# An AdaLN layer with spectral attention and routed experts on one core: sequences' constants from diagonal products, and row statistics and an epsilon moved to the activation engine

## The chip, the core and the metric

The kernel runs on one core of a Trainium2 chip. The engines are TensorE (PE: matrix products; PEld is its weight load), VectorE (DVE), ScalarE (ACT), GpSimd (POOL) and SyncE (SP, whose queue issues transfers). The metric is the time of one launch in microseconds on the device; the profile is of one execution of its own.

## The reference

The inputs are x of 4 sequences x 1024 tokens x 256 features, all float32. In short:

```python
mod = (silu(c) @ wmod).reshape(4, 6, 1, 256)          # sa, ca, ga, sb, cb, gb per sequence
ga, gb = (sign(g) * maximum(abs(g), 0.25) for g in (ga, gb))
h = layernorm(x) * (1 + ca) + sa
q, k, v = (unit(h @ W.T + b) for W, b in (...))       # unit(y): ifft(f / (|f| + 1e-8)), f = fft(y)
s = cumsum(ifft(fft(k) * fft(v)).real, axis=1)        # over the tokens of a sequence
x = x + ga * ifft(fft(s) * conj(fft(q))).real
h = layernorm(x) * (1 + cb) + sb
gate = h @ gate_w                                     # 8 experts, the best 2, softmax of their values
x = x + gb * sum(weight_e * expert_e(h))              # expert: clipped swiglu of 256 -> 2 x 512 -> 256
```

## The kernel before, in words

Transforms are products with a real 256 x 256 matrix (`fwd`: cosines, sines, the two real bins). They are folded into the weights: `gmat` is a weight times `fwd`, and what depends on a sequence (modulation, gates) is folded into a wide tile of constants for each of the four sequences, `batch` (2856 columns on 128 partitions). It has the projections of keys, values and queries with gate columns (`KV`, `Q`), the inverse transform with the gate `ga` in its columns (`INV`), and rows that are the same on all partitions: gate additions (`LOG`), `sb`, `1 + cb`, and `gb` times the experts' second bias (`SB`, `CB`, `GB2`). The first two sequences' tiles are filled in place. For the last two a tile `of` is filled, written to DRAM (`kept`, 1428 KB) and loaded later into one of the two `batch` buffers. `project_of` fills the projections, `gates_of` the rest; a row of `gb` also goes to `kept_gb`, from which expert blocks gather.

Tokens are worked through in 8 groups of 4 x 128 (`GT`), two groups a sequence, each group as two pairs of 2 x 128 (`PT`). `begin_group` takes the mean and variance of each row (`moments`: bn_stats and bn_aggr on DVE, then a square root on ACT and a reciprocal). `pair` is a generator of eight steps: normalise (`xn`) and transpose; project (L528) and square; magnitudes (`mag`: sum of two squares, square root, plus epsilon) and the product of keys and values; the queries' magnitudes; the running sum by products with a triangular matrix (L569 to L579); the product with the queries and a transpose (L594); the inverse transform (L604), the addition to x (L612), the second row statistics; and normalised rows into `row`. Two pairs are in work at a time. `route(g)` ranks the gates, finds each row's two slots (`slot_i`), and scatters rows into expert order in DRAM with eight indirect transfers on POOL's queue (L715); then it writes the group's first sums to the output (L737 to L746). `row` has two buffers, the x tiles three. `plan` makes blocks of 256 rows of one expert out of the slots that are full; `Block` loads rows and first weights, turns the rows (L881), and runs the expert (L918 to L962). The first block is started after group 2 is planned; blocks are then mixed with the remaining groups at a set rate.

The constants of sequence 0 stand before the first group. Those of the others are emitted by `prepare_later`, one step at every second step of the main loop from step 8 on (`LATER`), so between the pairs of groups 1 and on. PSUM has eight banks: three of tag `gv` (expert blocks), one `y`, and in `ps_m` two `in`, one `mid` and one `late`, which the constants share with the pairs.

The program text is not the order of an engine's queue: the tile framework's scheduler orders each engine's instructions when the program is built, by its own estimates and the data's order. Each engine then works through its queue strictly in that order, and waits there for what an instruction needs.

Of the kernel before, what the change touches and what calls it, by code (L numbers as in the profile page):

```python
# [7 lines left out]
FP = mybir.dt.float32  # L8
I32 = mybir.dt.int32
AF = mybir.ActivationFunctionType  # L10
ALU = mybir.AluOpType
AX = mybir.AxisListType

P = 128
# [5 lines left out]
GN = GT * P  # L20
RESERVE = 4
RARE = 2
LATER = 8
# [14 lines left out]
def adaln_layer_kernel(  # L38
# [56 lines left out]
    def late():  # L95
        return bank("late")

    x_tiles = {}

# [13 lines left out]
    eps_ln = const.tile([P, 1], FP, name="eps_ln")  # L113
    nc.gpsimd.memset(eps_ln, LN_EPS)
    tiny = const.tile([P, 1], FP, name="tiny")
    nc.gpsimd.memset(tiny, 1e-30)
# [77 lines left out]
    fwd = sp.tile([P, 2, D], FP, name="fwd")  # L194
    bwd = sp.tile([P, 2, D], FP, name="bwd")
    bq = sp.tile([P, 3, 2], FP, name="bq")
# [68 lines left out]
    )  # L265
    silb = sp.tile([P, 2, BATCH, P], FP, name="silb")

# [3 lines left out]
    gate_inv = sp.tile([P, 2, BATCH, NE], FP, name="gate_inv")  # L271
    gate_add = sp.tile([P, BATCH, NE], FP, name="gate_add")

    def gate_constants():
        pm = late()
        pmv = pm[:, : 6 * BATCH].rearrange("p (w h b) -> p w h b", w=3, h=2)
        for w in range(3):
            for h in range(2):
                for k in range(2):
# [6 lines left out]
                    )  # L286
        col = sp.tile([P, 3, 2, BATCH], FP, name="col")
        nc.vector.tensor_copy(col, pmv)
        size = sp.tile([P, 2, BATCH], FP, name="col_size")
        raw = col[:, 0]  # L290
# [42 lines left out]

    def project_of(b, t):


        rows_of = sp.tile([P, 2, P], FP, tag="rows_of", name="rows_of", bufs=2)
        nc.vector.tensor_copy(rows_of, lift[:, :, b : b + 1].to_broadcast([P, 2, P]))
        pu = bank("mid").rearrange("p (t n) -> p t n", n=D), bank("late")
        for n in range(3):  # L340
            u = pu[0][:, n - 1, :] if n else pu[1][:, :D]
            for h in range(2):
                nc.tensor.matmul(
                    u, lhsT=rows_of[:, h, :], rhs=gmat[:, h, n, :], start=(h == 0), stop=False
                )
            for k in range(2):
                nc.tensor.matmul(u, lhsT=bb[:, n, k], rhs=fwd[:, k, :], start=False, stop=(k == 1))
        for h in range(2):
            nc.vector.scalar_tensor_tensor(
                t[:, h * HC + KV : h * HC + Q].rearrange("p (t n) -> p t n", n=D),  # L350
                gmat[:, h, 1:3, :], mod[:, 1, h, b : b + 1], pu[0],
                ALU.mult, ALU.add,
            )
        for h in range(2):
            nc.vector.scalar_tensor_tensor(
                t[:, h * HC + Q : h * HC + Q + D], gmat[:, h, 0, :], mod[:, 1, h, b : b + 1],
                pu[1][:, :D],
                ALU.mult, ALU.add,
            )

    def gates_of(b, t):

        pg = late().rearrange("p (n d) -> p n d", n=2)
        for n, at in enumerate((2, 5)):
            for k in range(2):
                nc.tensor.matmul(
                    pg[:, n, :],
                    lhsT=silb[:, k, b, :],
                    rhs=wm[:, k, at * D : (at + 1) * D],
                    start=(k == 0),  # L370
                    stop=(k == 1),
                )
        raw = sp.tile([P, 2, D], FP, tag="raw", name="raw", bufs=1)
        nc.scalar.copy(raw, pg)
        size = sp.tile([P, 2, D], FP, tag="size", name="size", bufs=2)
        nc.vector.scalar_tensor_tensor(size, raw, -1.0, raw, ALU.mult, ALU.max)
        nc.vector.tensor_scalar(raw, raw, 0.0, 2.0, ALU.is_ge, ALU.mult)
        nc.vector.tensor_scalar(raw, raw, -1.0, None, ALU.add)
        nc.vector.scalar_tensor_tensor(size, size, 0.25, raw, ALU.max, ALU.mult)
        inv = t[:, INV:LOG].rearrange("p (c n) -> p c n", n=IC)  # L380
        nc.vector.tensor_mul(
            inv[:, :, :D], bwd, size[:, 0, :].unsqueeze(1).to_broadcast([P, 2, D])
        )
        nc.vector.tensor_copy(inv[:, :, D:], gate_inv[:, :, b, :])
        nc.vector.tensor_copy(
            t[:, : 2 * HC].rearrange("p (h n) -> p h n", n=HC)[:, :, 3 * D :], gate_in[:, :, b, :]
        )
        nc.vector.tensor_copy(t[:, LOG : LOG + NE], gate_add[:, b, :])
        pg = late()
        for k in range(2):  # L390
            nc.tensor.matmul(
                pg,
                lhsT=silb[:, k, b, :],
                rhs=wm[:, k, 3 * D : 5 * D],
                start=(k == 0),
                stop=(k == 1),
            )
        nc.scalar.copy(t[:, SB : SB + D], pg[:, :D])
        nc.vector.tensor_scalar(t[:, CB : CB + D], pg[:, D:], 1.0, None, ALU.add)
        nc.vector.tensor_mul(t[:, GB2 : GB2 + D], b2_sb, size[:, 1, :])  # L400
        nc.sync.dma_start(out=kept_gb[b : b + 1, :], in_=size[0:1, 1, :])

    t0 = batch_tile(0)
    project_of(0, t0)


    share = sp.tile([P, 2], FP, name="share")
    nc.vector.tensor_scalar(share, ident[:, 0 : P : P - 1], -1.0 / D, 2.0 / D, ALU.mult, ALU.add)
    pt = bank("in", 2).rearrange("p (c n) -> p c n", c=2)
    for c in range(2):  # L410
        for k in range(2):
            nc.tensor.transpose(
                pt[:, c, k * P : (k + 1) * P], fwd[:, k, c * P : (c + 1) * P], ident
            )
    for c in range(2):
        nc.scalar.activation(bwd[:, c, :], pt[:, c, :], AF.Copy, scale=share[:, c : c + 1])
    nc.vector.tensor_copy(silb, sil.unsqueeze(3).to_broadcast([P, 2, BATCH, P]))
    gate_constants()
    gates_of(0, t0)
    nc.vector.tensor_sub(strict, triu, ident)  # L420
# [8 lines left out]
    def prepare(b):  # L429

        t = sp.tile([P, COLS], FP, tag="of", name="of")
        project_of(b, t)
        gates_of(b, t)
        nc.sync.dma_start(out=kept[:, b], in_=t)

    def deviations(mv, tag):

        n = mv.shape[1]
        root = two.tile([P, n], FP, tag=tag + "root", name="root")
        r = two.tile([P, n], FP, tag=tag + "r", name="rstd")  # L440
        nc.scalar.activation(root, mv[:, :, 1], AF.Sqrt, bias=eps_ln)
        nc.vector.reciprocal(r, root)
        return root, r

    def moments(src, tag):
# [6 lines left out]
        for i in range(n):  # L452
            nc.vector.bn_aggr(mv[:, i, :], st[:, i, :])
        return mv

# [24 lines left out]
    def begin_group(g):  # L480

        x4 = x_tiles[g]
        mv = moments(x4, "a")
        root, r = deviations(mv, "a")
        nmr = two.tile([P, GT], FP, tag="nmr", name="nmr")
        nc.vector.tensor_mul(nmr, mv[:, :, 0], r)
        nc.vector.tensor_scalar(nmr, nmr, -1.0, 1.0, ALU.mult, ALU.add)
        gate = two.tile([P, GT, NE], FP, tag="gate", name="gate")
        row = rows.tile([P, GT, ROW], FP, tag="row", name="row")
        nc.gpsimd.tensor_copy(  # L490
            row[:, :, D + NE :].bitcast(I32),
            numbers[:, g * GT : (g + 1) * GT, :],
        )
        of_group[g] = root, r, nmr, gate, row

    def pair(g, j):
# [48 lines left out]
        def magnitudes(lo, hi, eng):  # L545
# [6 lines left out]
            nc.scalar.activation(mag[:, :, lo:hi, :], mag[:, :, lo:hi, :], AF.Sqrt, bias=tiny)  # L552
            nc.vector.tensor_scalar(mag[:, :, lo:hi, :], mag[:, :, lo:hi, :], EPS, None, ALU.add)

        magnitudes(1, 3, nc.vector)
        nc.vector.tensor_mul(mag[:, :, 1, :], mag[:, :, 1, :], mag[:, :, 2, :])
        nc.vector.reciprocal(mag[:, :, 1, :], mag[:, :, 1, :])
# [42 lines left out]

        po = bank("mid"), late()
        for k in range(PT):
            for h in range(2):
# [7 lines left out]
        for k in range(PT):  # L611
            nc.vector.tensor_add(xp[:, k, :], po[k][:, :D], xp[:, k, :])  # L612

# [3 lines left out]
            )  # L617
        mv2 = moments(xp, "b")
        _, r2 = deviations(mv2, "b")
        yield  # L620

# [5 lines left out]
        nmr2 = two.tile([P, PT], FP, tag="nmr2", name="nmr2")  # L627
        nc.vector.scalar_tensor_tensor(nmr2, mv2[:, :, 0], -1.0, r2, ALU.mult, ALU.mult)
        h_row = row[:, j : j + PT, :D]
        for k in range(PT):  # L630
# [386 lines left out]
    def prepare_later():  # L1017

        nonlocal mone, mtwo, tiny_ones, loads, slot_rows
        t1 = batch_tile(1)  # L1020
        project_of(1, t1)
        yield
        gates_of(1, t1)
# [20 lines left out]
    for t in range(NG * PER + STEPS - HALFWAY + 3):  # L1044
# [42 lines left out]
        if done_now is not None:  # L1087
            routes.append([done_now, 0, route(done_now)])
        if t >= LATER and t % 2 == 0:
            next(later, None)  # L1090
# [90 lines left out]
```

## Time and profile before

| | us |
|---|---|
| median of 3 runs | 809.25 (808.28 to 811.38) |
| the profiled execution | 811.83 |
| its span | 809.9 |
| PE busy | 694.5 (86%) |
| DVE busy | 554.7 (68%) |
| ACT busy | 326.8 (40%) |
| POOL busy | 390.7 (48%) |
| group 0, 1, 2: slots known | 100.7, 146.35, 194.97 |
| first expert block turned | 210.7 |

Busy times are shares of the whole span, and the kernel has two parts with different limits: until about 211 us it makes constants and works on four groups of tokens, after that it works on experts and the other four groups. So a share is to be read by stretch. In rows of groups of instructions, "x8 | 14.1, 1757 | 0.0" means eight instructions, 14.1 us in all, 1757 ns each, and the idle time of the engine before them, with what ended it. An arrow `<-` in such a row stands between what is written and what is read. In rows by time the first two numbers are start and length in us.

### The profile page before, as it was taken

How to read it: one execution, taken by the hardware profiler on the slowest of the kernel's cores; microseconds unless marked ns; L12 is line 12 of the kernel's file. 1: busy time of each engine (PE TensorE's matmuls, PEld its weight loads, DVE VectorE, ACT ScalarE, POOL GpSimd, SP SyncE). 2: the span in 40 equal slices, each digit the busy share in tenths (PEclk: the TensorE clock that was granted, in tenths of full speed). 3: DMA queues.
4: the chain of work that ended last, by engine and by line, in shares of the span. 5: the costliest groups of instructions: out<-in, count | busy, mean ns of one | idle time of the engine just before them, and what ended most of it. 6: DMA issues, size and time to landing. Idle time of an engine off the chain costs nothing. (4 is left out here: it accounts for less than half of the span.)

```text
span 809.9 us, 10038 instructions
## 1 busy us (share of the span) xinstructions
PE 694.5 (86%) x2876; PEld 533.6 (66%) x2876; DVE 554.7 (68%) x1570; ACT 326.8 (40%) x606; POOL 390.7 (48%) x391
## 2 busy tenths in 40 slices
PE   6989796596697879799899897979968999999991
PEld 5655553353475657677587675758756888888881
DVE  3678979869366767878697867766925656655650
ACT  4435336153364626464566363534211332232230
POOL 1023143414354664666567656646755545555432
PEclk9989999585599879999899898989978999999996
DMA  9300041310762248327532752275876655755422
GB/s 312 131 0 1 18 174 60 122 57 32 237 179 53 47 124 284 79 54 219 130 84 61 228 133 31 69 207 140 168 217 175 143 144 165 181 166 168 91 40 26
DMA packets 55553, 100.16 MB, mean 124 GB/s; under 512 B 7165, under 2 KB 40586, under 8 KB 54986
## 3 DMA queue, kind: packets, MB, share of 16 engines
q1 hardware_dynamic: 38218, 72.68, 26.4%
q0 software_dynamic: 17280, 26.83, 18.9%
q8 instruction: 25, 0.41, 0.2%
q14 instruction: 30, 0.25, 0.1%
HBM read 72.80 MB, written 27.99 MB: 124 GB/s over the span
## 5 line engine op out<-in xcount | busy, mean ns | idle before, releaser
L918 PE MATMUL gv<-xt,w 128*128 128x256 f32 x1184 | 281.9, 392 | 11.8 <-DVE gt L930 7.8
L918 PEld LDWEIGHTS gv<-xt,w 128*128 128x128 f32 x1184 | 228.9, 197 | 48.3 <-DVE gt L930 9.6
L962 POOL DMA_INDIRECT out_dram<-gb,token x74 | 120.1, 1624 | 61.9 <-DVE gb L958 45.2
L948 PE MATMUL py<-w_sb,h 128*128 x592 | 137.2, 385 | 1.0 <-DVE gb L958 1.0
L901 POOL DMA_INDIRECT gb<-kept_gb,token x74 | 81.0, 1094 | 105.7 <-DVE gt L930 28.2
L934 ACT ACTIVATE sg<-gt 128x512 f32<-128x512 f32 x74 | 46.6, 630 | 206.2 <-DVE gt L930 169.2
L948 PEld LDWEIGHTS py<-w_sb,h 128*128 128x128 f32 x592 | 112.9, 192 | 18.0 <-DVE gb L958 1.4
L528 PE MATMUL in<-batch,ht 128*128 128x512 f32 (+1 forms) x256 | 99.1, 534 | 5.8 <-ACT ht L516 5.8
L715 POOL DMA_INDIRECT slots<-row,slot_i x64 | 67.3, 1052 | 51.5 <-DVE slot_i L710 24.3
L930 DVE TENSOR_SCALAR gt<-gv,bias 128x256 f32<-128x256 f32 x148 | 65.0, 474 | 24.0 <-PE gv L918 18.1
L528 PEld LDWEIGHTS in<-batch,ht 128*128 128x128 f32 x256 | 50.0, 205 | 44.0 <-issue 30.9
L942 POOL TENSOR_TENSOR h<-vt,sg 128x512 f32<-128x512 f32 x42 | 55.1, 1316 | 49.4 <-DVE vt L941 40.6
L937 ACT ACTIVATE vt<-gv,bias 128x256 f32<-128x256 f32 x148 | 61.5, 463 | 16.9 <-PE gv L918 15.6
L940 DVE TENSOR_SCALAR vt<-vt 128x512 f32<-128x512 f32 x74 | 34.2, 462 | 45.9 <-ACT vt L937 42.3
L547 POOL COPY mag<-sq 128x4 f32<-128x4 f32 (+1 forms) x64 | 21.3, 390 | 79.6 <-ACT sq L537 69.1
L941 DVE TENSOR_TENSOR vt<-vt,gt 128x512 f32<-128x512 f32 x74 | 51.9, 701 | 1.6
L958 DVE SCALAR_TENSOR_TENSOR gb<-py,weight,gb 128x256 f32<-128x256 f32 x74 | 32.7, 476 | 25.0 <-PE py L948 16.5
L535 ACT COPY z<-in 128x512 f32<-128x512 f32 (+1 forms) x64 | 29.5, 479 | 49.6 <-PE in L528 46.6
L563 POOL TENSOR_TENSOR z<-z,mag 128x512 f32<-128x512 f32 x16 | 20.6, 1284 | 47.2 <-DVE mag L562 36.0
L594 PE MATMUL mid<-msk,u 128*128 128x128 f32 x64 | 14.1, 328 | 31.9 <-DVE u L472 23.8
L737 PE MATMUL late<-batch,w_t 8*128 8x256 f32 x64 | 23.8, 502 | 15.1 <-ACT w_t L733 8.9
L451 DVE BATCH_NORM_STATS2 st<-x 128x6 f32<-128x256 f32 x64 | 24.3, 412 | 17.2 <-DMA x<-in_x_dram 17.2
(213 smaller groups left out, 1006.6 us busy)
## 6 DMA issues: line engine op xcount, KB each, us to landing
w<-in_w1t_dram SPq DMA_DIRECT2D x37, 1024.0 KB
x_in<-slots SPq DMA_DIRECT2D x37, 266.0 KB
x<-in_x_dram SPq DMA_DIRECT2D x8, 512.0 KB
w_sb<-in_w2t_dram SPq DMA_DIRECT2D x1, 4096.0 KB
out_dram<-x SPq DMA_DIRECT2D x8, 512.0 KB
kept<-of SPq DMA_DIRECT2D x2, 1428.0 KB
batch<-kept SPq DMA_DIRECT2D x2, 1428.0 KB
slots<-fill SPq DMA_DIRECT2D x9, 266.0 KB
```

Source lines behind the costliest of these rows:

```text
L528: nc.tensor.matmul(pz, lhsT=ht[:, h, k * P : (k + 1) * P], rhs=pb[:, h * HC + lo : h * HC + hi], start=(h == 0), stop=(h == 1),)
L715: s = nc.gpsimd.indirect_dma_start(out=slots, out_offset=bass.IndirectOffsetOnAxis(ap=slot_i[:, n, i : i + 1], axis=0), in_=row[:, i, :], ...
L901: nc.gpsimd.indirect_dma_start(out=self.gb[:, i, :], out_offset=None, in_=kept_gb, in_offset=bass.IndirectOffsetOnAxis(ap=self.token[:, i, ...
L918: nc.tensor.matmul(pp[:, j, :], lhsT=self.w1[:, h, s, f * P : (f + 1) * P], rhs=self.xt[:, h, :], start=(h == 0), stop=(h == 1),)
L930: nc.vector.tensor_scalar(gt[:, j], ps[0][:, j], self.bias[:, self.k, 0, f : f + 1], LIMIT, ALU.add, ALU.min)
L934: nc.scalar.activation(sg, gt, AF.Sigmoid, scale=ALPHA)
L937: nc.scalar.activation(vt[:, j], ps[1][:, j], AF.Identity, bias=self.bias[:, self.k, 1, f : f + 1])
L940: nc.vector.tensor_scalar(vt, vt, LIMIT + 1.0, 1.0 - LIMIT, ALU.min, ALU.max)
L941: nc.vector.tensor_mul(vt, vt, gt)
L942: self.eng.tensor_mul(self.h[:, 2 * pair : 2 * pair + 2, :], vt, sg)
L948: nc.tensor.matmul(py[:, i, :], lhsT=self.h[:, f, i * P : (i + 1) * P], rhs=w2_sb[:, bass.ds(self.e, 1), f, :].rearrange("p a d -> p (a d) ...
L962: s = nc.gpsimd.indirect_dma_start(out=out, out_offset=bass.IndirectOffsetOnAxis(ap=self.token[:, i, 0:1], axis=0), in_=y[:, i, :], in_off ...
```

## The change

1. Sequences' constants. `silb` (silu(c) spread over 128 columns) and `bwd` (the inverse matrix) are gone. The four sequences' gate rows are made at once on 4 partitions (`gate_rows`), and so is what is added to the projections (`project_rows`). A row is spread over the partitions by a product with `pick_row` (ones in row b). The scaling of `gmat`'s and `fwd`'s rows becomes a product with a diagonal matrix that ACT makes (`diagonals`). Results go to PSUM banks of tag `gv` (`spare`), and ACT copies them into the tile. Sequence 0's projections are made as before (`project_first`); its gates are emitted at step 3 of the main loop. Small column copies go to POOL (`gate_columns`). The rows of `gb` are written by one transfer.
2. Row statistics of groups 0 to 2 (`EARLY = 3`). The second ones take the sum from the addition to x (an accumulating output), then a square about the mean on ACT, whose output also accumulates; the row tile is the scratch. Groups 1 and 2 take the first statistics by two ACT passes a row block (Copy and Square, both accumulating), again with the row tile as scratch. Group 0's first ones and groups 3 to 7 stay with bn_stats.
3. Epsilon of the magnitudes. The values' epsilon is folded into the product of two magnitudes (one three-operand instruction). The others are added on ACT for groups 0 to 2, and on DVE as before for the rest.

```diff
+EARLY = 3
+    def spare():
+        return ps_gv.tile([P, 512], FP, tag="gv", name="spare")
...
+    def gate_rows():
+        nc.gpsimd.tensor_copy(
+            pick_row, ident[:BATCH, :BATCH].unsqueeze(2).to_broadcast([BATCH, BATCH, P])
+        )
+        pg = spare(), spare()
+        for at, to in ((5 * D, pg[0][:BATCH, :D]), (3 * D, pg[1][:BATCH])):
             for k in range(2):
                 nc.tensor.matmul(
-                    pg[:, n, :],
-                    lhsT=silb[:, k, b, :],
-                    rhs=wm[:, k, at * D : (at + 1) * D],
+                    to,
+                    lhsT=sil[:, k, :],
+                    rhs=wm[:, k, at : at + to.shape[1]],
...
+        nc.sync.dma_start(out=kept_gb[:BATCH, :], in_=size)
+        nc.scalar.copy(of_all[:, :D], pg[1][:BATCH, :D])
+        nc.scalar.activation(of_all[:, D : 2 * D], pg[1][:BATCH, D:], AF.Copy, bias=1.0)
...
+    def diagonals(columns):
+        t = sp.tile([P, 2, P], FP, tag="diag", name="diag", bufs=2)
+        for h in range(2):
+            nc.scalar.activation(t[:, h, :], ident, AF.Copy, scale=columns[:, h])
+        return t
+
+    def project_of(b, t):
+        diag = diagonals(mod[:, 1, :, b : b + 1])
+        for h in range(2):
+            pu = spare()
+            nc.tensor.matmul(
+                pu, lhsT=pick_row[:, b, :], rhs=added_of[:, : 2 * D], start=True, stop=False
+            )
+            nc.tensor.matmul(
+                pu, lhsT=diag[:, h, :], rhs=gmat[:, h, 1:3, :].rearrange("p t n -> p (t n)"),
+                start=False, stop=True,
+            )
+            nc.scalar.copy(t[:, h * HC + KV : h * HC + Q], pu)
...
+    def gate_columns(b, t):
         inv = t[:, INV:LOG].rearrange("p (c n) -> p c n", n=IC)
-        nc.vector.tensor_mul(
-            inv[:, :, :D], bwd, size[:, 0, :].unsqueeze(1).to_broadcast([P, 2, D])
-        )
-        nc.vector.tensor_copy(inv[:, :, D:], gate_inv[:, :, b, :])
+        nc.gpsimd.tensor_copy(inv[:, :, D:], gate_inv[:, :, b, :])
...
+    def gates_of(b, t):
+        diag = diagonals(size_col[:, :, b : b + 1])
+        pi = spare().rearrange("p (c n) -> p c n", c=2)
...
+            nc.scalar.activation(t[:, at : at + D], pi[:, c, :], AF.Copy, scale=share[:, c : c + 1])
+        pg = spare()
+        nc.tensor.matmul(
+            pg, lhsT=pick_row[:, b, :], rhs=of_all[:, : 2 * D], start=True, stop=True
+        )
+        nc.scalar.copy(t[:, SB : SB + 2 * D], pg)
...
+        nc.vector.tensor_mul(t[:, GB2 : GB2 + D], b2_sb, pg[:, :D])
...
+    def moments_act(src, total, junk, tag):
+        n = src.shape[1]
+        mv = two.tile([P, n, 2], FP, tag=tag + "mv", name="mv")
+        minus = mv[:, :, 0]
+        nc.vector.tensor_scalar(minus, total, -1.0 / D, None, ALU.mult)
+        for i in range(n):
+            nc.scalar.activation(
+                junk[:, i, :], src[:, i, :], AF.Square,
+                bias=mv[:, i, 0:1], accum_out=mv[:, i, 1:2],
+            )
+        return minus, *inverse_root(mv[:, :, 1], 1.0 / D, tag)
...
+        if 0 < g < EARLY:
+            total = two.tile([P, GT], FP, tag="atotal", name="total")
+            for i in range(GT):
+                nc.scalar.activation(
+                    row[:, i, :D], x4[:, i, :], AF.Copy, accum_out=total[:, i : i + 1]
+                )
+            mean, root, r = moments_act(x4, total, row[:, :, :D], "a")
+        else:
+            mean, root, r = moments(x4, "a")
...
-            nc.vector.tensor_scalar(mag[:, :, lo:hi, :], mag[:, :, lo:hi, :], EPS, None, ALU.add)
+            if g < EARLY:
+                nc.scalar.activation(
+                    mag[:, :, lo, :], mag[:, :, lo, :], AF.Identity, bias=eps_mag
+                )
+            else:
+                nc.vector.tensor_scalar(
+                    mag[:, :, lo, :], mag[:, :, lo, :], EPS, None, ALU.add
+                )
...
-        nc.vector.tensor_mul(mag[:, :, 1, :], mag[:, :, 1, :], mag[:, :, 2, :])
+        nc.vector.scalar_tensor_tensor(
+            mag[:, :, 1, :], mag[:, :, 2, :], EPS, mag[:, :, 1, :], ALU.add, ALU.mult
+        )
...
+            if g < EARLY:
+                nc.vector.scalar_tensor_tensor(
+                    xp[:, k, :], po[k][:, :D], 1.0, xp[:, k, :], ALU.mult, ALU.add,
+                    accum_out=total[:, k : k + 1],
+                )
...
         t1 = batch_tile(1)
+        project_rows()
+        yield
         project_of(1, t1)
-        yield
+        gate_columns(1, t1)
         gates_of(1, t1)
         yield
...
+        if t == 3:
+            gate_rows()
+            gates_of(0, t0)
```

## The prediction

> **What bounds the kernel now.** I read the page's head and its 40 slices first, to find the stages, and then the busy time by stretch, cut where the trace shows an event: 25 us (first projection), 101, 146 (groups 0 and 1 have their slots), 211 (first expert block turned).
>
> ```profile
> span 809.9 us, 10038 instructions
> ...
> PE   6989796596697879799899897979968999999991
> ...
> DVE  3678979869366767878697867766925656655650
> ACT  4435336153364626464566363534211332232230
> ```
> ```profile
> 25.00:101.00 76.00, 66.07 (x238) 42.60 (x238) 62.18 (x174) 31.71 (x60) 14.84 (x26) 0.93 0.04 14
> 101.00:146.00 45.00, 34.40 (x124) 21.68 (x123) 39.03 (x105) 21.08 (x39) 16.56 (x23) 0.91 0.29 109
> 146.00:211.00 65.00, 44.86 (x116) 24.19 (x116) 48.83 (x175) 22.84 (x44) 27.02 (x33) 0.66 0.25 79
> 211.00:810.00 599.00, 532.02 (x2316) 429.94 (x2314) 393.85 (x1067) 241.71 (x446) 329.94 (x291) 0.93 0.52 135
> ```
> A row is length, then busy time of PE, PEld, DVE, ACT, POOL, then TensorE's granted clock. To 101 PE and DVE are both full (66 and 62 of 76), to 146 DVE (39 of 45); ACT is under half busy. From 211 on PE bounds (532 of 599). The change works in the first 211 us, and what it wins there moves the whole PE-bound part forward: the first block needs group 2's plan, and nothing after 211 has a time of its own to wait for.
>
> Then the groups of instructions of 0 to 210 by form:
>
> ```profile
> L451 DVE BATCH_NORM_STATS2 st<-x 128x6 f32<-128x256 f32 x34 | 13.1, 412 | 8.8 <-DMA x<-in_x_dram 8.8
> ...
> L376 DVE SCALAR_TENSOR_TENSOR size<-raw 128x512 f32<-128x512 f32 x4 | 4.3, 1087 | 1.6 <-ACT raw L374 1.6
> ...
> L553 DVE TENSOR_SCALAR mag<-mag 128x516 f32<-128x516 f32 x8 | 3.4, 420 | 2.1 <-ACT mag L552 2.0
> ```
> ```profile
> L505 ACT ACTIVATE xn<-x,nmr,rstd 128x256 f32<-128x256 f32 x16 | 8.5, 591 | 2.8 <-DVE nmr L487 2.8
> L552 ACT ACTIVATE mag<-mag,tiny 128x258 f32<-128x258 f32 x8 | 4.1, 512 | 7.6 <-POOL mag L551 7.6
> ```
> Neighbours on DVE overlap by 0.07 to 0.09 us (the 0.42 us L472 and L473 start 0.33 apart), on ACT likewise, so I count start to start. PE's queue gives its price:
>
> ```profile
> 65.14 1.03 PE L343 MATMUL mid<-gmat,rows_of 128*128 128x256 f32 x4
> 66.01 1.03 PE L347 MATMUL mid<-fwd,bb 128*128 128x256 f32 x4
> ```
> Four records, two products of 256 columns, start 0.87 before the next four: 0.43 us a product at full clock, in proportion to the width.
>
> **The change part by part.** *Sequences' constants.* DVE loses silb 0.7, three rows_of 0.7, six L349 at 0.65 = 3.9, six L355 at 0.4 = 2.4, L376 to L379 four times 9.2, L381 2.6, L399 1.4, and twelve small copies (to POOL) 1.1: 22.0. It gains four operations on 4 partitions, 1.1 (by the 256-wide rows). Net -21. ACT loses raw, L398 and bwd, 4.3, and gains 14 diagonals (128 wide; between the 128x4 row's 0.30 and 0.51 at 258; 0.3 taken), evictions of projections 3 x 1.7, of gates 4 x 1.3, rows 2.0: net +12. PE gains nothing: a sequence took 16 products of 256 and 2 of 512 columns, 8.6 us; now 4 of 512, 4 of 256 and 4 of 128 with spreads of 512 and 256, 7.3, and once 5.2 for the 12 four-row products of the projections (as wide as before) and 2.6 for those of the gates. They now use the three gv banks, idle before the first block, not "late" and "mid". POOL gets 12 copies (0.17 each, as L490), pick_row and bqb, in stretches where it idles 61 of 76.
>
> *Row statistics.* DVE loses 12 + 8 bn_stats (0.345) and as many bn_aggr (0.087), 8.6, and gains eight 0.09 scalings; the 12 residual adds become three-operand ones (0.48 for 0.42). Net -7. ACT gains 8 + 8 passes for groups 1 and 2 and 12 for the pairs: 28 at 0.52, 14.6.
>
> *Eps.* For six pairs both L553 go to ACT: -3.3 on DVE, +12 x 0.43 = 5.2 on ACT. Groups 3 to 7 save 0.14 a pair behind a bounding PE: nothing counted; uncovered it is 1.4.
>
> Two rules are weighed here. An add with ACT: L553 at 128x258 is 0.28 on DVE, L552 of that size 0.51 on ACT. The Trainium skill (ScalarE: Activation LUTs, Rules for kernel authors) sends add and mul to VectorE, because ScalarE is slower by the element. By the rule alone the eps makes 12 x 0.23 = 2.8 us more work, and if ACT bounds it is 5.2 us lost; by the stretches above DVE is at 82% and ACT at 42%, and it is 3.3 won. I take the trace, but keep the rule for the sum below, where ACT is full. Accumulating outputs: no row of before has one. The Trainium skill (VectorE: DVE Perf Modes, Two Vector instructions with no wait between them) counts such an operation as two instructions, the second reading the accumulator. The smallest DVE rows (0.15) and ACT rows (part, 0.2) bound that read; below, nothing. DVE 0 to 1.8, ACT 0 to 5.6 in all; no gain is possible, as the pass itself is unchanged. I take nothing on DVE (small ops show 0.08 start to start) and 0.1 on ACT, +2.8.
>
> Together to 211: DVE 161 - 31 = 130, ACT 85 + 35 = 120, PE as it was. The gain is not 31.
>
> *25 to 101.* Of the -31 about 20 fall here (14.5 constants, 3.5 group statistics, 1.7 pairs, 1.9 eps, less 1.7 of new work): DVE 62 to 42. ACT gains 19 (22 less 3): 32 to about 50. PE's products from L280 (23.0) to the first L682 (97.5) are 57 us at full clock by widths, 77% of that time; half-clock slices (0.93) and 10 us of waits are the rest. In the changed order of the built program the same stretch has 138 products, 60 us. So PE is now the fullest: at once 83.3, at 95% and one half-clock slice (3 us) 89.5. Gain 8 (3 to 13, the upper end if half of the 5% left goes too).
>
> *101 to 146.* DVE 39 to 31 (constants -7, pairs and eps -3.7, group 3's bn_stats come forward from 154, +1.8), ACT 21 to 34. But here a wait is new. Group 2's sums use its row tile as scratch, and that pool has two buffers: the first pass waits until all eight scatters of group 0 have landed.
>
> ```profile
> 101.00 1.18 POOL L715 DMA_INDIRECT slots<-row,slot_i  x1 [14.26 <-DVE slot_i L710]
> ...
> 110.87 0.97 POOL L715 DMA_INDIRECT slots<-row,slot_i  x1 [0.30 <-issue]
> ...
> 113.60 0.19 POOL L490 COPY row<-numbers 128x8 int32<-128x8 int32 x1 [0.50 <-DMA slots<-row,slot_i]
> ```
> From slots known (100.7) to a free tile is 13 us. In the changed order ACT has 8 us of work before it, so ACT stands some 5 us, and behind the wait stand group 2's statistics (4.2), xn, ht and its z: xn at about +18.5 instead of +6 us, first product at +25 instead of +20.6 (121.27). POOL's copies into the fourth sequence's tile stand ahead of these scatters and wait until the third's 1428 KB are written (at most 5.6 us: issued 99.82, L355 written 105.4), mostly behind 4.7 us of ACT work. x3's bn_stats now follow the last add into x0 (L745) by 2.4 us of DVE work, and x3's load needs that buffer written out first: L745 ended at 122.6, the load was issued at 125.55, and x4's took 3.4 to its reader, so DVE stands up to 4 us there; it would otherwise stand for group 2's product, so nothing is added. From the product to group 1's slots 25 us become 17.4 of DVE work, at 88% 20. Gain 1.
>
> *146 to 211.* DVE loses 2.2 of pair statistics, 1.3 of eps, and 3.5 of bn_stats of x3 and x4, which now stand elsewhere, and with x4's the 5.4 us wait for its load. x3's statistics no longer hold back pair 6: its product came 31 us after pair 5's (139.8 to 171.2) with 22 of DVE work; now there are 16.5, so 20 to 24. Against it each pair's second statistics pass ACT (two passes, +0.7) and the eps (+0.5) in the chain. Gain 6 to 9, with the last 22 us from pair 7's product to the block unchanged: 7 taken.
>
> SP: x2's load now stands behind the one write of gate rows, some 25 us in instead of 13.7; its reader is past 85. Three other row writes go. Sum: 8 + 1 + 7 = 16. The profiled execution took 811.8 (span 809.9 and 1.9 around it), 2.6 above the median of 809.25 of the runs shown: 795.8 on it, 793 by the median.
>
> **The rivals.** *PE and the row wait keep most of it* (17%). For: PE was at 77% of pure work in the first stretch and gets 3 us more; the wait of group 2 leaves PE a gap, in which its clock can halve, as it did in 146 to 211. First stretch 3, second -4, third 7: 803. Against: half of PE's waits there name DVE's constants, which go.
>
> *The saving comes through* (17%). For: constants leave DVE's queue from between the pairs, PE's half-clock slices go, the x4 wait and pair 6's delay go fully. 13 + 4 + 11 = 28: 781. Against: the row wait, which nothing removes.
>
> *Slower* (9%): ACT's queue. ACT stands behind PE's diagonal products, and PE behind three banks that ACT alone empties, between the pairs' own evictions. The place is 25 to 101, the price ACT's idle time: now 44 of 76. With 50 of work the stretch breaks even at 26 idle. At 36 it takes 86, +10; the row wait adds 4.5, the last stretch gives 6 back: 818. Against: most of those 44 us are waits for queues that shorten.
>
> *Nothing measurable* (9%): the new waits and the later gain cancel, 809.
>
> **How the numbers follow.** The sum has 48%, 786 to 799. With the first and second rival (799 to 805, 773 to 786) that makes 82% faster; 9% within 0.5% (4 us, about what a measurement of this kernel can tell from no change), 9% slower. 777 to 805 leaves out the best third of the second rival and the last two cases, about two in ten.
>
> **What would show it.** First turn at 190 to 199 instead of 210.7; DVE busy to there near 130, ACT near 120; PE over 90% busy from 25 on until group 0's slots, which come at 88 to 97; ACT waiting about 5 us on the landing of slots before group 2's sums; the x4 wait of 5.4 gone; 599 us from the first turn to the end within 3. The reasoning is wrong if ACT passes 95% before 90 us, if the accumulating passes take over 0.75 us each, or if the part behind the first turn grows by what the front wins.

## The result and the profile after

The changed kernel took 808.0 us (median of 20 runs, 800.2 to 823.4), the kernel before 809.4 in runs beside it (20, 805.5 to 814.0); the ratio is 0.9954, 95% interval [0.9932, 0.9977]. Measured again later it was 0.9977 [0.9945, 1.0009]. Runs more than 1.5% above a kernel's fastest are left out of a ratio; the changed kernel spreads so widely that this takes some of its own slower runs away, and the medians of all runs (808.0 and 809.4, then 811.8 and 810.3) are closer still. 793 had been forecast, with a range of 777 to 805.

The page of the changed kernel, its 40 slices:

```profile
span 808.4 us, 10073 instructions
...
PE   6999985776598789799799898989879999999991
...
DVE  3567254968658776878597759785844655655650
ACT  4645556834265635554566354634221333232220
...
PEclk9988896988599889989999799999999999999996
```

The busy time by the same stretches as before (length; then PE, PEld, DVE, ACT, POOL; then the granted clock):

```profile
25.00:101.00 76.00, 73.15 (x231) 37.34 (x231) 40.02 (x107) 42.37 (x95) 14.34 (x29) 0.87 0.08 31
101.00:146.00 45.00, 33.07 (x109) 18.24 (x108) 25.73 (x75) 26.83 (x67) 15.51 (x24) 0.85 0.23 85
146.00:211.00 65.00, 44.40 (x140) 25.63 (x138) 54.90 (x190) 33.17 (x67) 29.52 (x40) 0.86 0.20 73
211.00:810.00 599.00, 529.87 (x2316) 428.60 (x2316) 394.16 (x1076) 242.83 (x447) 330.62 (x291) 0.93 0.52 136
```

VectorE did lose its 31 us: summed to 211 it is 130.0 where it was 160.8. The front is nevertheless not shorter. PE is busy 73 of the first 76 us, at a granted clock of 0.87 instead of 0.93. By the events that cut the stretches (the start of the cast into slot_i, by which a group's slots are known, and the first turn of an expert block), in the two profiled executions, before and after:

- slots of group 0 at 100.5, then 104.6: 4.0 lost;
- from there to the slots of group 1, 45.7, then 51.3: 5.6 lost;
- to the slots of group 2, 48.6, then 42.2: 6.4 won;
- first turn at 210.7, then 213.5; from it to the end 599.2, then 594.9.

Two places in the trace carry the losses. The first is PE's queue where the constants of one sequence are made:

```profile
69.21 1.12 PE L429 MATMUL spare<-added_of,pick_row 4*128 4x512 f32 x2
70.26 1.12 PE L432 MATMUL spare<-gmat,diag 128*128 128x512 f32 x2
71.31 1.12 PE L429 MATMUL spare<-added_of,pick_row 4*128 4x512 f32 x2
72.36 1.60 PE L432 MATMUL spare<-gmat,diag 128*128 128x512 f32 x2
73.89 1.22 PE L439 MATMUL spare<-added_of,pick_row 4*128 4x256 f32 x2
75.04 1.22 PE L442 MATMUL spare<-gmat,diag 128*128 128x256 f32 x2
```

Each row is one product of the program in two records. By the kernel before (0.87 for two products of 256 columns) they should start 0.86 apart; the first start 1.05 apart. At 72.9 the clock falls to half for 13.7 us, and 256 columns take 1.15. The second place is ScalarE's wait for the row buffer, and what PE did after it:

```profile
114.63 0.56 ACT L847 COPY w_t<-late 8x512 f32<-8x512 f32 x1
120.94 0.42 ACT L574 ACTIVATE row<-x 128x256 f32<-128x256 f32 x1 [5.75 <-DMA slots<-row,slot_i]
121.26 0.19 ACT L574 ACTIVATION_READ_ACCUMULATOR row<-x 128x1 f32 x1
121.35 0.40 ACT L574 ACTIVATE row<-x 128x256 f32<-128x256 f32 x1
...
124.86 0.35 ACT L689 COPY s<-mid 128x256 f32<-128x256 f32 x1
```
```profile
97.13 5.43 PE L621 MATMUL in<-batch,ht 128*128 128x512 f32 x16
...
127.26 1.08 PE L696 MATMUL mid<-msk,u 128*128 128x128 f32 x3 [8.39 <-DVE nmr L582]
...
130.09 7.62 PE L621 MATMUL in<-batch,ht 128*128 128x512 f32 x16 [0.68 <-ACT ht L609]
```

The wait is 5.75 us. ScalarE takes its work in order: the copy L689 of another pair, whose product had ended at 117.8, ran only at 124.86, behind the wait and group 2's eight passes. PE, whose next work needs what VectorE makes of that copy and group 2's scaled rows, stood 8.39 us, and the 16 records that follow ran in part at half clock (from 120.7 to 134.3) and took 7.62 us; at full clock the same line took 5.43.

### The profile page after: what moved, and what is told of

Read it like the earlier page. It is cut to its first block, busy times and chain, and to the rows that moved or that the text cites. A ratio compares the mean times of both kernels' runs of the same rounds, so it can differ in the third digit from the quotient of the medians.

```text
span 808.4 us, 10073 instructions
## 1 busy us (share of the span) xinstructions
PE 698.0 (86%) x2880; PEld 524.6 (65%) x2880; DVE 524.2 (65%) x1490; ACT 356.9 (44%) x704; POOL 393.2 (49%) x406
## 5 line engine op out<-in xcount | busy, mean ns | idle before, releaser
L1032 PE MATMUL gv<-xt,w 128*128 128x256 f32 x1184 | 284.9, 394 | 18.0 <-DVE gt L1044 10.7
L1062 PE MATMUL py<-w_sb,h 128*128 x592 | 135.1, 381 | 1.0 <-DVE gb L1072 1.0
L621 PE MATMUL in<-batch,ht 128*128 128x512 f32 (+1 forms) x256 | 100.5, 540 | 4.2 <-ACT ht L609 3.5
L621 PEld LDWEIGHTS in<-batch,ht 128*128 128x128 f32 x256 | 50.2, 207 | 45.2 <-issue 34.9
L1054 DVE TENSOR_SCALAR vt<-vt 128x512 f32<-128x512 f32 x74 | 34.9, 472 | 48.5 <-ACT vt L1051 43.9
L640 POOL COPY mag<-sq 128x4 f32<-128x4 f32 (+1 forms) x64 | 18.8, 352 | 85.2 <-ACT sq L630 72.9
L1055 DVE TENSOR_TENSOR vt<-vt,gt 128x512 f32<-128x512 f32 x74 | 54.2, 732 | 1.6
L696 PEld LDWEIGHTS mid<-msk,u 128*128 128x128 f32 x64 | 9.0, 161 | 40.7 <-issue 37.7
L995 PE MATMUL turned<-msk,x_in 128*128 128x128 f32 x148 | 23.4, 282 | 10.4 <-DMA x_in<-slots 10.4
```

What stands on the lines that cost most here:

```text
L621: nc.tensor.matmul(pz, lhsT=ht[:, h, k * P : (k + 1) * P], rhs=pb[:, h * HC + lo : h * HC + hi], start=(h == 0), stop=(h == 1),)
L1032: nc.tensor.matmul(pp[:, j, :], lhsT=self.w1[:, h, s, f * P : (f + 1) * P], rhs=self.xt[:, h, :], start=(h == 0), stop=(h == 1),)
L1054: nc.vector.tensor_scalar(vt, vt, LIMIT + 1.0, 1.0 - LIMIT, ALU.min, ALU.max)
L1055: nc.vector.tensor_mul(vt, vt, gt)
L1062: nc.tensor.matmul(py[:, i, :], lhsT=self.h[:, f, i * P : (i + 1) * P], rhs=w2_sb[:, bass.ds(self.e, 1), f, :].rearrange("p a d -> p (a d) ...
```

## The experiments

The theory was that two costs ate the gain: spread products of 4 rows among products of 128 (with a clock that falls under them), and the row wait. Its rivals: ScalarE's in-order queue; or simply the number of products. Each ratio is to the kernel before in the same set of runs. That kernel's median was 804.2 us in the first set (the first four experiments), 810.3 in the second (the next four) and 802.4 in the third, so ratios of different sets are compared with less certainty than those of one.

**One part at a time, and one cost at a time.** The constants alone:

```
-EARLY = 3
+EARLY = 0
```


> The constants' part alone (EARLY = 0, so all row statistics and the eps of the first magnitudes are back on VectorE; the fold of eps into the product of two magnitudes stays). Theory (the products of 4-row spreads and the lower clock under them cost TensorE what VectorE is spared): no gain, 808 to 814 us, ratio to the kernel before 1.000 to 1.006; the slots of group 0 at 103 to 106 us, the first turn at 211 to 216. Rival (ScalarE's in-order queue, with the statistics' passes ahead of evictions, holds the front up): without those passes the constants show their gain, 800 to 804 us, ratio 0.988 to 0.993, first turn near 203.

Measured 1.0006 [0.9981, 1.0031]: no gain, as the theory had it, and not what ScalarE's queue would make. But the profiled execution (802.6 us) has the slots of group 0 at 96.3 and the first turn at 205.0, far better than forecast, with no half clock in the constants' block. Its runs go from 799 to 819, as widely as the changed kernel's. The last experiment comes back to this.

The statistics and the eps alone (the kernel before with `moments_act`, the accumulating residual add and `eps_mag`):

> The statistics and the eps alone, with the constants as in the kernel before. Theory: the stretch of the third group gets its 6.5 us and loses up to 4 to the wait for the row buffer; 804 to 807 us, ratio 0.993 to 0.997, slots of group 0 near 100, first turn 206 to 209. Rival (ScalarE's queue): the added 20 us of passes hold evictions up and it is no faster than before, 809 to 813, ratio 1.000 to 1.005, with TensorE's waits for ScalarE longer than in the kernel before.

Measured 1.0085 [1.0059, 1.0110]: slower than before, which the theory had not forecast, and more than the rival had. The row wait is longer here:

```profile
111.40 0.42 ACT L504 ACTIVATE row<-x 128x256 f32<-128x256 f32 x1 [8.35 <-DMA slots<-row,slot_i]
```

The slots of group 1 come at 152.2 and those of group 2 at 199.4, both later than before.

A tile for what nobody reads:

```
+    junk = sp.tile([P, GT, D], FP, name="junk")
...
-                    row[:, i, :D], x4[:, i, :], AF.Copy, accum_out=total[:, i : i + 1]
+                    junk[:, i, :], x4[:, i, :], AF.Copy, accum_out=total[:, i : i + 1]
...
-            mean, root, r = moments_act(x4, total, row[:, :, :D], "a")
+            mean, root, r = moments_act(x4, total, junk, "a")
```


> The changed kernel with a tile of its own for what the two statistics passes of groups 1 and 2 write and nobody reads, instead of the row buffer whose scatters are under way. Theory (the row wait costs the second stretch about 4 of its 5.6 us): the wait of 5.75 us of ScalarE is gone, slots of group 1 at 151 to 153 us, first turn near 209 to 210, 803 to 805 us, ratio 0.992 to 0.995. Rival (TensorE, fed by the constants of sequence 3, is what fills that stretch): the wait goes and the slots of group 1 stay within 1 us of 155.9, 807 to 809 us.

Measured 0.9937 [0.9910, 0.9964]. The wait is gone, and the slots of group 1 come at 137.1, the first turn at 200.8, 14 and 8 us earlier than forecast. 8 us of that are the half clock in the constants' block, which this execution, like that of the constants alone, does not have (slots of group 0 at 96.6). At the slots of group 1 the edit also removes more than the wait: with a tile of its own group 2's passes need not stand behind the scatters, and the scheduler put them 78 us earlier.

```profile
43.20 0.42 ACT L575 ACTIVATE junk<-x 128x256 f32<-128x256 f32 x1
```

In the changed kernel the first of them starts at 120.94. So the row buffer had kept not only a wait of 5.75 us in this stretch but also the 4.0 us of the passes behind it. The interval overlaps with those of the changed kernel's two ratios, so by itself this does not show a gain; the medians of all runs differ more, 800.0 to 804.2 of the kernel before, against 811.8 to 810.3.

Spreads of full height, the added rows zero:

```
-    of_all = sp.tile([BATCH, 3 * D], FP, name="of_all")
+    of_all = sp.tile([P, 3 * D], FP, name="of_all")
+    nc.gpsimd.memset(of_all, 0.0)
...
-    pick_row = sp.tile([BATCH, BATCH, P], FP, name="pick_row")
+    pick_row = sp.tile([P, BATCH, P], FP, name="pick_row")
```
(added_of likewise; only the first BATCH rows are written.)

> The changed kernel with the spread rows and the picking matrix kept at 128 partitions, the added ones zero, so that each spread product loads weights of the same height as the diagonal product beside it; the number and the width of the products stay, and two memsets on POOL come in. Theory (a 4-row product among 128-row ones costs about 0.2 us more than its width and keeps the clock from rising): products of 512 columns start 0.86 us apart in place of 1.05, the half-clock slice at 72.8 us goes, slots of group 0 at 99 to 101 us, 801 to 804 us, ratio 0.989 to 0.993. Rival (the number of products, not their height, fills TensorE): starts as far apart as now, slots of group 0 within 1 us of 104.6, 807 to 809 us.

Measured 0.9919 [0.9896, 0.9941]. The same products, with zeros added:

```profile
65.93 1.02 PE L431 MATMUL spare<-added_of,pick_row 128*128 128x512 f32 x2
66.78 1.02 PE L434 MATMUL spare<-gmat,diag 128*128 128x512 f32 x2
67.64 1.02 PE L431 MATMUL spare<-added_of,pick_row 128*128 128x512 f32 x2
```

They start 0.86 apart, there is no half clock between 11.8 and 103.9 us, and the slots of group 0 come at 91.2 (99 to 101 had been expected). The number of products is the same, so the rival that counts them falls.

**Do the two costs add up?** Both edits together; the statistics alone with a tile of their own, by the same edit; the constants alone at full height; and the changed kernel beside them on the same chip.

> The changed kernel with both: full-height spreads and picking matrix, and a tile of its own for the unread outputs of the two statistics passes of groups 1 and 2. Theory (two separate costs, the 4-row products before the slots of group 0 and the row wait between those of groups 0 and 1): they add up; slots of group 0 near 91 us, of group 1 at 131 to 134, first turn 186 to 190, ratio to the kernel before 0.982 to 0.987, 5 to 8 us below the changed kernel's time on the same chip twice over. Rival (one bound behind both, the half clock that comes whenever TensorE has been full for a time): no better than the better of the two alone, ratio 0.990 to 0.993, first turn 193 or later.

> The statistics and the eps alone, constants as in the kernel before, with a tile of its own for the unread outputs. Theory (the row wait of 8.35 us is what made the statistics alone slower than the kernel before): ScalarE waits no more there, 7 to 11 us less than the statistics alone, ratio to the kernel before 0.994 to 1.000. Rival (the added passes and accumulator reads in ScalarE's queue are what costs): within 2 us of the statistics alone, ratio 1.005 to 1.010.

> Full-height spreads, and the constants' part alone (EARLY = 0). Theory: 5 to 7 us less than the constants alone with 4-row spreads, ratio to the kernel before 0.990 to 0.995, slots of group 0 at 91 to 93 us; VectorE's statistics stay in the third stretch, so the part from the slots of group 1 to those of group 2 stays at 45 to 48 us. Rival (height does not matter without the statistics on ScalarE): ratio 0.999 to 1.002.

> The changed kernel itself, beside the others on the same chip. Both theories: ratio to the kernel before 0.993 to 0.998, as in its first measurement; its place among the others says what each of them is worth.

Measured: both edits 0.9830 [0.9801, 0.9858], a version that beats both kernels (median 796.3, the kernel before 810.3, the changed one 811.8). Statistics with scratch 0.9894 [0.9861, 0.9927]; constants at full height 0.9892 [0.9856, 0.9928], with the slots of group 0 at 89.2; the changed kernel 0.9977. The two parts alone came out a little better than forecast.

So each part is worth 1.1% once its own cost is taken out, and each was worth nothing or less with it: from 1.0006 to 0.9892 by the height of the spreads, from 1.0085 to 0.9894 by the tile of its own. (Both steps go from the first set to the second.) Together they give 1.7%, less than 2.2. The added passes on ScalarE are all still there, so it is not their work in ScalarE's queue that costs, but the place where they stood and waited. The version with both has in its stretches:

```profile
25.00:101.00 76.00, 74.00 (x288) 43.50 (x287) 52.17 (x144) 57.98 (x139) 23.38 (x45) 1.00 0.15 55
101.00:146.00 45.00, 32.47 (x95) 18.96 (x94) 33.39 (x113) 21.97 (x47) 16.85 (x26) 0.79 0.23 77
```

Full clock in the first, with 288 records where the changed kernel got 231 done in the same 76 us; and ScalarE, in spite of 58 us of work there, does not hold PE up. Its slots come at 89.9, 132.6 and 179.6 and its first turn at 195.1 (186 to 190 was expected: the third stretch gives less than in the changed kernel, see below).

**Is it the change of height, or the 4-row product itself?** On the version with own scratch, the spreads of one sequence put one after the other:

```
+        for h in range(2):
+            nc.tensor.matmul(
+                pk[h], lhsT=pick_row[:, b, :], rhs=added_of[:, : 2 * D], start=True, stop=False
+            )
+        nc.tensor.matmul(
+            pu, lhsT=pick_row[:, b, :],
+            rhs=added_of[:, 2 * D :].unsqueeze(1).to_broadcast([BATCH, 2, D]),
+            start=True, stop=False,
+        )
+        for h in range(2):
+            nc.tensor.matmul(
+                pk[h], lhsT=diag[:, h, :], rhs=gmat[:, h, 1:3, :].rearrange("p t n -> p (t n)"),
+                start=False, stop=True,
+            )
...
```


> The 4-row spreads of project_of put one after the other, ahead of the diagonal products of the same sequence (three banks; the two query spreads become one product of 512 columns), on top of the tile of its own for the unread outputs. Changes between 4-row and 128-row weights fall from 8 to 2 for each sequence; columns are the same. Theory A (each change of height costs 0.2 us, and nothing else matters): a 4-row product behind a 4-row one starts 0.86 us after it, two sequences ahead of the slots of group 0 save 2.4 us, slots near 94, ratio to the kernel before 0.989 to 0.993. Theory B (what counts for the clock is columns times rows in a slice of 3.41 us): 2.6 us of 4-row products in a row leave a slice nearly unfilled, half clock follows for one or two slices in each sequence, slots at 97 to 102, ratio 0.996 to 1.004. Theory C (a 4-row product itself costs 0.2 us more): products stay 1.05 us apart, slots within 1 us of 96.5, ratio 0.992 to 0.995.

Measured 0.9930 [0.9901, 0.9958], within the noise of own scratch alone (0.9937). The starts at full clock:

```profile
80.18 1.98 PE L431 MATMUL spare<-added_of,pick_row 4*128 4x512 f32 x4
82.00 1.02 PE L434 MATMUL spare<-added_of,pick_row 4*128 4x512 f32 x2
82.95 1.98 PE L440 MATMUL spare<-gmat,diag 128*128 128x512 f32 x4
84.77 1.03 PE L447 MATMUL spare<-gmat,diag 128*128 128x256 f32 x4
```

A 4-row spread behind another costs no 0.19 more: three of 512 columns take 2.77 (2.58 by width), and the two diagonal products behind them 1.82 (1.72). What is left, 0.1 us at a time, stands on either side of a change of height, and theory C falls. From the first spread to the product behind the block (L701 at 88.10) the sequence took 7.92 us; ungrouped it is 9.09, at full height 7.51, so the height costs a sequence 1.6 us. Where the time goes is seen in the weight loads. First ungrouped, then at full height, the same products of 256 columns:

```profile
84.43 0.30 PEld L443 LDWEIGHTS spare<-gmat,diag 128*128 128x128 f32 x2 [0.33 <-issue]
85.06 0.29 PEld L440 LDWEIGHTS spare<-added_of,pick_row 4*128 4x128 f32 x2 [0.33 <-issue]
```
```profile
79.67 0.41 PEld L444 LDWEIGHTS spare<-gmat,diag 128*128 128x128 f32 x2
80.10 0.41 PEld L441 LDWEIGHTS spare<-added_of,pick_row 128*128 128x128 f32 x2
```

Where the height changes, the load starts with its own product (84.44 and 85.06 are the products' starts), although it waits for no other engine. Between equal heights it runs 0.2 us ahead (L444's product starts at 79.89). The Trainium skill (TensorE: Matmul & The Clock Gate, Step-by-step: what each phase is for) says that loads are pulled ahead of running products where row groups don't conflict or the background buffer takes them, and that the row count does not matter to a load's time. The second holds for the load itself (two 4-row loads 0.29, two of 128 rows 0.30). The first is seen between equal heights; at a change of height the pull-ahead is lost, at some 0.2 us a product.

Yet the grouped version won nothing: the half clock of theory B came too, if less of it than B had. In its profiled execution the clock was at half for a slice at 71.9 and again at 99.2, behind the first and the third of the three blocks of spreads, and the slots of group 0 came at 96.0, 0.6 us ahead of those with own scratch alone. Ratio and slots are thus those of theory C, by two effects that nearly cancel and not by its mechanism.

**The clock by itself.** On the version with both edits, 24 products of 512 columns that nobody reads, in one block; only the height differs:

```
+            for _ in range(24):
+                nc.tensor.matmul(unread, lhsT=pick_row[:BATCH, 0, :], rhs=of_all[:BATCH, : 2 * D], start=True, stop=True)
```


> The kernel with full-height spreads and own scratch, and 24 added products of 512 columns in one block behind the shared gates of sequence 0, with weights and data of 4 rows, into a bank that nobody reads. Theory (a product of 4 rows hardly counts as work for the clock): after a slice or two at full clock the block runs at half clock to its end, 24 products take 35 to 41 us. Rival (the clock asks only whether TensorE is busy): no half-clock slice in the block, 24 times 0.86 is 20.6, with 0.2 for the changes of height 21 us.

> The same block with 128 rows of weights and data, of which all but 4 are zeros, so that the numbers multiplied are the same. Both theories: full clock throughout, 20.5 to 21 us for the block. Were it at half clock too, neither height nor rows but the zeros would be what the clock sees.

The block with 4 rows and the same with 128:

```profile
40.84 36.00 PE L1213 MATMUL spare<-of_all,pick_row 4*128 4x512 f32 x48
```
```profile
38.97 20.76 PE L1213 MATMUL spare<-of_all,pick_row 128*128 128x512 f32 x48
```

And the granted clock, by windows around the two blocks (4 rows, then 128):

```profile
41.00:77.00 36.00, 36.00 (x49) 13.87 (x50) 2.30 (x4) 5.34 (x21) 0.94 (x1) 0.57 0.00 0
```
```profile
39.00:60.00 21.00, 21.00 (x50) 9.29 (x49) 2.53 (x4) 5.57 (x21) 1.17 (x1) 1.00 0.00 0
```

PE has work without a gap in both. With 4 rows the clock falls 5.4 us into the block, at 46.3, and stays at half to its end; with 128 rows, nearly all zeros, it stays full. So the clock does not ask whether TensorE is busy but how much of its height is used, and 4 rows hardly count. The width of the output does not matter: in the second version only products of 128 rows with 4 output columns (L410, L414) run from 69.1 to 74.5 us, and the clock stays full.

I worked the same out for all 14 profiled executions. Their clock changes only after whole multiples of 3.41 us (72.9 to 86.5 is four), so time falls into slices of that length. At full clock a slice holds about 4,096 columns (eight records of 512, 0.43 us apart). For every slice I took the columns streamed in it, each record's spread evenly over its shown time, times its rows over 128, as a share of those 4,096. If that share is under 0.37 the next slice is at half clock, else at full: of 2,696 slices at full clock this names the wrong successor for 5, of 549 at half clock for 3. Counting products of 4 and 8 rows like any other, the best edge is wrong for 59 of the 2,696. The edge also says why one poor slice became four in the changed kernel: a slice at half clock holds 0.5 at most, and the four have 0.29, 0.31, 0.09 and only then 0.47. These shares are estimates from the records. The Trainium skill (TensorE: Matmul & The Clock Gate, Part 1: The HAM clock gate) has free-running windows of 3,413 ns and a clock set by how busy TensorE has been. The slices here have that length; "busy" has to be read by rows.

**Where the slices fall.** Last, the changed kernel once more:

> One more profile of the changed kernel. Theory (the slices of 3.41 us run freely, so where they fall against the constants' block differs from one execution to the next, and the block is near the edge): with slices that begin elsewhere the half clock at 72.5 to 86 us can be missing, and then the slots of group 0 are at 96 to 98 us; with slices that begin within 0.5 us of the two profiles so far it is there and they are at 104. Rival (something in the program pulls the clock down there): half clock at 72 to 87 us and slots at 104 to 105 wherever the slices begin.

Its slices begin at 67.4 and 70.8 us, where those of the two profiles so far began at 69.5 and 69.2. It took 803.2 us (the kernel before has a median of 802.4 in this set). The same 14 us, in this execution and in the changed kernel's first profile:

```profile
72.00:86.00 14.00, 14.00 (x46) 6.55 (x45) 9.05 (x28) 8.15 (x18) 2.72 (x3) 1.00 0.00 0
```
```profile
72.00:86.00 14.00, 14.00 (x29) 7.14 (x28) 8.33 (x25) 6.30 (x15) 2.79 (x3) 0.53 0.00 0
```

46 records of PE against 29, slots of group 0 at 96.9 against 104.6 (96 to 98 had been expected), first turn at 204.2 against 213.5. By the share above, the two slices of this execution in which the block begins are at 0.43 and 0.40, just over the edge of 0.37; in the first two profiles the slice is at 0.35 and 0.31. One program, two fronts 8 us apart in the first stretch, by where slices that the program does not set happen to lie. It may explain the wide spread of the changed kernel and of the constants alone; that is not shown, and how often each happens three profiles cannot say.

## Why the prediction was wrong

- *VectorE loses 31 us to 211: right.* 160.8 to 130.0. *ScalarE gains 35: nearly.* 85.1 to 114.1. The accumulator read, bounded by 0 and 0.2 and taken at 0.1, starts 0.09 us ahead of the next pass (121.26 and 121.35 above); on VectorE, where it was taken as nothing, it is a record of 0.08 us (L717).
- *"PE gains nothing": the step that failed.* It priced every product by its width, from rows in which all weights were 128 high (L343, L347). Ten changes of height in a sequence cost 1.6 us together. The price stood in the profile of before, in the 8-row products of a group's first sums:

```profile
118.03 1.13 PE L737 MATMUL late<-batch,w_t 8*128 8x256 f32 x4
119.09 0.66 PE L594 MATMUL mid<-msk,u 128*128 128x128 f32 x4
```

Four records of 256 columns are 0.86 us by width; from their start to that of the 128-row products behind them it is 1.06. By the slots of group 0 the height costs 5.7 us (last profile of the changed kernel 96.9, full height 91.2), 6.7 (own scratch 96.6, with full height 89.9) or 7.1 (constants alone, 96.3 and 89.2); this holds slices at half clock (6.8 us from 37.9 with own scratch, behind the 4-row spreads of the shared gates) that full height does not show. Where the slices lie badly it is nearly 8 more.

- *25 to 101, gain 8: was +3.7 or -4.0.* With full-height spreads it is 9.3 to 11.4. "At 95% and one half-clock slice" foresaw one slice of 3 us; a block of 13.7 at half clock came out of the added products themselves, not from idling. The kernel before was profiled once, and that execution has half clock from 25.5 to 28.9 and from 49.4 to 56.2; its front may vary too, so gains against it are sure to a few us only.
- *101 to 146, gain 1: was -5.6.* The wait was sized well (5 us forecast, 5.75 measured). What stands behind it was not: group 2's scaled rows came 22.7 us behind the slots of group 0 instead of 18.5, and the square of its first projection (L630; the forecast's "first product" is the time of that line in before, 121.27) 32 instead of 25. PE stood 8.39 us and then ran the 16 records of L621 in 7.62 us instead of 5.43. I had named a halved clock behind that gap in a rival and left it out of the sum. With a tile of its own, which takes away the wait and the 4.0 us of passes, this stretch is 40.5 instead of 50.7 (own scratch against the last profile of the changed kernel) and 42.7 instead of 52.0 (full height with and without).
- *146 to 211, gain 7: 6.8 to the first turn, but not for the reason given alone.* The wait of 5.4 us for x4's load is gone, as forecast. But with both edits the same stretch wins only 2.0. VectorE's saving is there in both: between the slots of groups 1 and 2 it is busy 38.5 us before, 33.9 in the changed kernel, 34.9 with both edits. With both edits it stands 8.5 us once for the copy of a projection (z, L631), and TensorE's clock is 0.75 there instead of 0.85; why was not traced further. Over the last two stretches together 8 us were forecast; the changed kernel wins 1.2, the version with both edits 4.9. With the statistics alone the third stretch is the same with the row buffer and without (62.6 and 62.9 us), and the second shows the whole cost (54.7 and 45.1).
- *A shorter front moves the PE-bound part forward: right in the main.* From the first turn to the end all versions lie between 593 and 605 us, a wider band than the 3 us forecast, and not in the order of their fronts.
- *The rivals.* "PE and the row wait keep most of it", 803 us, was the nearest, with both mechanisms named but the price of the products at 3 us; its stretches of 3, -4 and 7 are close to the 3.7, -5.1 and 7.9 of the changed kernel's last profile. "Slower: ACT's queue" was wrong in kind: between 74 and 82 us ScalarE waited for PE's products (4.01 us before L445), not PE for ScalarE.

With the two failed terms taken out on the chip, the first turn comes 15.6 us earlier, and the ratio gives 1.7% (13.8 us of 809.4), where the sum had 16. That these agree is in part luck: the stretches gave 10.7, 3.0 and 2.0 instead of 8, 1 and 7, and the sum of 16 still had the cost of the wait in it.

## What to carry to other kernels

Width alone prices a product only among neighbours of one height: before work is moved onto TensorE as thin products, ask what height stands beside them, look in the trace at hand for products of another height, and pad with zero rows where the columns are paid anyway. Where a pass is run for its accumulated output alone, its written output still has an owner, which can hold the pass back as well as make it wait: give it a scratch tile that no transfer reads. And where two parts of one change are measured together, take each apart with its own cost removed; here two gains of 1.1% lay under costs of 1.1% and 1.9%.

## What was not expected of the hardware

- Alternating 4-row and 128-row weights costs 0.2 us for each product (1.05 instead of 0.86 us for 512 columns); the weight load does not run ahead of the running product there. Products of 8 rows show the same in the kernel before.
- The granted clock follows columns times rows: 24 products of 512 columns take 20.76 us with 128 rows and 36.00 with 4, although PE never pauses.
- The same program had the slots of its first group 8 us earlier or later by where the clock's slices of 3.41 us began, as its block of constants lay near the edge (0.31 to 0.43 of a full slice, the edge being at 0.37).
